# A planner's idea of TensorE and of the shared PSUM bank, corrected in a four-layer kernel

## The chip, the cores and the metric

The kernel runs on one core of one Trainium2 chip. The metric is the device time of one execution in microseconds. The kernel before takes 14,381.78 us in the median of three timed runs (14,376.06 to 14,391.36). Besides, one execution was recorded by the hardware profiler; all durations below come from it.

The core has five instruction queues, each worked off in order: PE (TensorE, matmuls), DVE (VectorE), ACT (ScalarE), POOL (GpSimd) and SP (SyncE, which only issues DMAs). The engines meet through semaphores.

## The reference

Four images of 64 x 64 positions with 128 channels (x is 4 x 64 x 64 x 128, f32) go through four layers. Layers 0 and 1 are state-space blocks: projections, a depthwise 3x3 convolution, and then a scan over all 4096 positions in four directions, with 16 states for every channel:

```
x_dbl = einsum('bkdl,kcd->bkcl', xs, x_proj_w)      # xs: the sequence in 4 directions
dts, Bs, Cs = split(x_dbl)                          # R rows, 16 rows, 16 rows
delta = softplus(einsum('bkrl,kdr->bkdl', dts, dt_w) + dt_b)
h = exp(delta * A) * h + (delta * x) * B            # one step of the scan, for each state
y = sum over the 16 states of h * C
```

The sums of the four directions are normalised, gated and projected. Layer 0 has 128 inner channels (R = 4) and a side branch of two full 3x3 convolutions; layer 1 has 256 inner channels (R = 8) and an MLP behind it. Layer 2 is a gated message from nine neighbours with two small MLPs, layer 3 a 7x7 neighbourhood attention. The change touches layers 0 and 1 alone.

## The kernel before, in words

Layers 0 and 1 of all images are computed in one stage, `scan_layers`. Its main line, `Scans.run` (L556), walks through 3072 units: 12 tasks (an image, a layer and a block of 128 channels), in each 16 steps (a direction and 1024 positions), in each step 16 units of 8 channels x 16 states on 128 partitions. For unit u the main line records: the DVE scan of unit u (L449) and, after every second unit, the DVE product with C (hc, L459); the POOL product of unit u+3 (h from dub and repB, L430); two bf16 matmuls and an exponential on ACT for unit u+2 (da, L438 and L440); every second unit the sums over states (yps, L530); now and then copies of y, the state and C on ACT. At the end of each unit's recording it issues the load of dub for unit u+7 on SP (L423). da has two PSUM buffers, so the matmuls of unit u+2 wait until scan u is done.

Two further streams of work are recorded in between, piece by piece, as Python generators wrapped in a `Lane`:

- **Preparation** (`Scans.prepare`, L314), lane "prep". It begins 22 units (`AHEAD`) before its step is used and has the 16 units of one step to finish; a slot r of a preparation is the unit r after its beginning. It projects xs into xd (f32 matmuls into ms, read by an ACT copy), stores xd to DRAM as xdd and loads it back repeated as repB and repC. Then it computes delta for two halves: a matmul into ms, read by an Abs (low) and a Relu (delta) on ACT; Exp, Ln, a sum on POOL make the softplus; a POOL product makes low = delta * x, which is stored to DRAM as dud (L388), from where every dub is loaded. Last it splits delta into three bf16 parts (parts), which twelve small DMAs (`own`, L400) copy into dp, the right-hand side of the decay matmuls. Of a second block of channels of the same image (`t.first` set) the projection is taken over from the first.
- **Side work** (`Side`), lane "side": everything else of layers 0 and 1, for other images than the one being scanned: projections, Silu with its two table loads, normalisations, depthwise and full convolutions, the MLP. Nearly all its matmuls are 512 columns wide, in f32.

Both streams share a single PSUM bank, tile ms (`bufs=1`, got through `bank()`, which makes the lane the `holder`). A matmul into ms must wait until ACT has read what was there; the holder is given up when the piece that reads it has been recorded.

What goes out when is decided by a planner at build time. `Plan` keeps for PE, ACT and POOL the time at which each would be done with what has been recorded (`at`), with a cost per instruction from `Counted` (all preparation and side instructions are recorded through it, at L97 in the profile). `Plan.slot` moves its clock by `UNIT` = 3.6 us per unit and books the main line's own work. Each generator yields a hint which engines its next piece uses ("PE", "ACT", "PE POOL", "TAB" for an activation with table loads); `Lane.fits` says yes if each of them could start early enough: start + `USUAL` must lie within the current slot plus `SLACK`. `Lane.ready` is the planned end of the lane's previous piece. `Lane.blocked` keeps a piece back that needs the bank while the other lane holds it; `Lane.step` first makes the holder record on until it lets go.

Preparation's pieces go out in a slot while they fit, and are forced out, fitting or not, while `pieces.count < rest - 1`, where `rest` is the slot r of the preparation. Side pieces go out as a credit allows, which grows by at least 0.83 pieces per unit; the longer they did not fit, the more lateness is allowed (0.06 us per piece of credit, up to 50 pieces).

Stores and reloads are not issued at once: `Plan.post` keeps them until the planned end of what they store (or a given due time) has passed, so that SP, which works in order, does not stand in front of the dub loads. Before the first dub load of a step all posts of "prep" are issued; at `rest == 0` all of "prep" and "rep".

Of the kernel before, what the change touches and what calls it, by code (L numbers as in the profile page):

```python
# [9 lines left out]
F32 = mybir.dt.float32  # L10
# [7 lines left out]
P = 128  # L18
# [10 lines left out]
HALVES = TS // T  # L29
# [44 lines left out]
class Counted:  # L74
# [5 lines left out]
    def __getattr__(self, name):  # L80
        call = getattr(self.engine, name)
        kind = self.kind

        def counted(*args, **kw):
            out = kw.get("out", args[0] if args else None)
            if kind == "PE":

                lhs, rhs = args[1:3]
                us = (4.0e-3 if rhs.dtype == F32 else 1.0e-3) * columns(rhs) * columns(lhs) / P
            elif kind == "ACT":  # L90
                us = 1.3 if name == "preload_act_table_set" else 0.2 + 0.85e-3 * columns(out)
                if kw.get("func", args[2] if len(args) > 2 else None) in (AF.Silu, AF.Gelu):
                    us += 1.3
            else:
                us = (1.0e-3 if name.startswith("tensor_scalar") else 2.3e-3) * columns(out)
            self.plan.enter(kind, us)
            return call(*args, **kw)  # L97

        return counted


def columns(t):
    return int(np.prod(t.shape[1:]))


UNIT = 3.6
USUAL = dict(PE=2.1, ACT=0.7, TAB=3.3, POOL=1.3)
SLACK = dict(PE=1.2, ACT=2.2, POOL=3.0)
LANDING = 8.0
FOUR_LANDING = 12.0  # L110
# [3 lines left out]
class Plan:  # L114
# [3 lines left out]
    def __init__(self, nc):  # L118
        self.nc = nc
        self.at = dict(PE=0.0, ACT=0.0, POOL=0.0)  # L120
        self.now, self.done = 0.0, 0.0
        self.posted, self.running = [], False

        self.lanes, self.holder = {}, None
        self.tensor = Counted(nc.tensor, self, "PE")
        self.scalar = Counted(nc.scalar, self, "ACT")
        self.gpsimd = Counted(nc.gpsimd, self, "POOL")
        self.vector, self.sync = nc.vector, nc.sync
# [36 lines left out]
class Lane:  # L165
# [4 lines left out]
    def __init__(self, plan, name, gen):  # L170
        self.plan, self.name, self.gen = plan, name, gen
        plan.lanes[name] = self
        self.next, self.ready, self.count = "", 0.0, 0

    def blocked(self):

        first = self.count == 0 or self.next.startswith("PE")
        return first and self.plan.holder not in (None, self.name)

    def fits(self, more=0.0):  # L180

        plan = self.plan
        if self.blocked():
            return False
        for what in self.next.split():
            if what == "SP":
                return self.ready <= plan.now
            kind = "ACT" if what == "TAB" else what
            start = max(plan.at[kind], self.ready)
            if start + USUAL[what] > plan.now + UNIT + SLACK[kind] + more:  # L190
                return False
        return True

    def step(self):

        plan = self.plan
        while self.blocked():
            plan.lanes[plan.holder].step()
        plan.done = max(self.ready, plan.now)
        reads = "ACT" in self.next or "TAB" in self.next  # L200
        try:
            self.next = next(self.gen)
        except StopIteration:
            return False
        finally:
            if reads and plan.holder == self.name:
                plan.holder = None
        self.ready = plan.done
        self.count += 1
        if isinstance(self.next, tuple):  # L210
            self.next, landed = self.next
            self.ready = max(self.ready, landed)
        return True
# [51 lines left out]
class Scans:  # L265
# [34 lines left out]
    def fetch(self, t):  # L300
# [6 lines left out]
        for c in range(NSTEP):  # L307
            for i, xc in enumerate(t.xc):
                cols = slice(c * TS, (c + 1) * TS)
                self.nc.sync.dma_start(out=xc[:, cols], in_=t.xcd[i][:, cols])  # L310
                yield

    def prepare(self, t, step):

        nc, W, half, post = self.plan, t.W, self.half, self.plan.post
        begin = self.plan.now
        k, c = t.steps[step]
        R = W.rank
        rows = R + 2 * NS

        xd = self.tile("xd", 1, shape=(P, T))
        if t.first is None:
            xdd = t.xdd[step] = self.dram.tile(
                [rows, TS], F32, name="xdd", tag=f"xdd{W.layer}", bufs=(4, 2 * len(t.steps))[W.layer]
            )
            ps = self.bank()
            for ti in range(W.nct):
                for i in range(HALVES):
                    nc.tensor.matmul(
                        image(ps[i * H : (i + 1) * H, :]),  # L330
                        W.xp[:, ti, k, :],
                        self.view(t.xc[ti], k, c, i, HALVES),
                        start=ti == 0,
                        stop=ti == W.nct - 1,
                    )
                yield "PE" if ti + 1 < W.nct else "ACT"
            nc.scalar.copy(xd, ps)

            def store_xd():
                for i in range(HALVES):  # L340
                    nc.sync.dma_start(out=xdd[:, half(i)], in_=xd[i * H : i * H + rows, :])

            post("prep", store_xd)
            ready = max(self.plan.done, self.plan.now) + LANDING
            yield "PE"
        else:
            xdd, ready = t.first.xdd[step], begin
            for i in range(HALVES):
                nc.sync.dma_start(out=xd[i * H : i * H + R, :], in_=xdd[0:R, half(i)])
            yield "PE", self.plan.now + LANDING  # L350
        out = t.prepared[step] = {}

        def repeat(i):
            rep = out["BC"[i]] = self.tile("rep" + "BC"[i], 2 - i)
            src = bass.AP(xdd.tensor, xdd.offset + (R + i * NS) * TS, [[TS, NS], [0, 8], [1, TS]])
            nc.sync.dma_start(out=rep, in_=src)

        for i, free in enumerate((5, 8)):
            post("rep", lambda i=i: repeat(i), max(begin + free * UNIT, ready))

        bias = W.dtb[:, k, t.ct : t.ct + 1]
        delta, low = self.tile("delta", 1), self.tile("low", 1)
        for i in range(HALVES):
            ps = self.bank()
            nc.tensor.matmul(
                ps,
                W.dtw[i * H : i * H + R, k, t.ct * P : (t.ct + 1) * P],
                xd[i * H : i * H + R, :],
                start=True,
                stop=True,  # L370
            )
            yield "ACT"
            nc.scalar.activation(low[:, half(i)], ps, AF.Abs, bias=bias)
            nc.scalar.activation(delta[:, half(i)], ps, AF.Relu, bias=bias)
            yield "PE" if i + 1 < HALVES else "ACT"
        nc.scalar.activation(low, low, AF.Exp, scale=-1.0)
        yield "ACT"
        nc.scalar.activation(low, low, AF.Ln, bias=1.0)
        yield "POOL"
        nc.gpsimd.tensor_add(delta, delta, low)  # L380
        yield "ACT POOL"
        parts = self.tile("parts", 1, shape=(P, 3, TS), dtype=BF16)
        nc.scalar.copy(parts[:, 0, :], delta)
        nc.gpsimd.tensor_mul(image(low), image(delta), self.view(t.xc[t.ct], k, c, 0, 1))
        yield "POOL"
        t.x_done = step == len(t.steps) - 1
        dud = out["du"] = self.dram.tile([P, TS], F32, name="dud", tag="dud", bufs=3)
        post("prep", lambda: nc.sync.dma_start(out=dud, in_=low))  # L388
        nc.gpsimd.tensor_sub(delta, delta, parts[:, 0, :])
        yield "ACT"  # L390
        nc.scalar.copy(parts[:, 1, :], delta)
        yield "POOL"
        nc.gpsimd.tensor_sub(parts[:, 2, :], delta, parts[:, 1, :])


        def own(part, j):
            if j == part == 0:
                out["delta"] = self.tile("dp", 2, shape=(96, 4, TS), dtype=BF16)
            nc.sync.dma_start(
                out=out["delta"][32 * part : 32 * part + 32, j, :], in_=parts[32 * j : 32 * j + 32, part, :]  # L400
            )

        for i in range(12):
            j, part = divmod(i, 3)
            post("rep", lambda part=part, j=j: own(part, j), begin + (9 + 0.7 * i) * UNIT)
        yield ""
# [143 lines left out]
    def run(self, between):  # L550

        total = NU * len(self.tasks)
        first = self.tasks[0]
# [6 lines left out]
        pieces, fetch, fetched = Lane(self.plan, "prep", iter(())), iter(()), 0  # L560
        for u in range(-7, total):
# [20 lines left out]
            ahead, rest = divmod(u + AHEAD, NG)  # L582
# [4 lines left out]
            if rest == 0 and 0 < ahead < total // NG:  # L587
# [7 lines left out]
                pieces = Lane(self.plan, "prep", self.prepare(self.tasks[n], step))  # L595
# [2 lines left out]
            if step == 0 and fetched < n < len(self.tasks) and self.tasks[n - 1].x_done:  # L598
                fetch, fetched = self.fetch(self.tasks[n]), n
            next(fetch, None)  # L600
            while (pieces.count < rest - 1 or pieces.fits()) and pieces.step():
                pass
            if u >= 0:
                n, i = divmod(u, NU)
# [1421 lines left out]
```

## Time and profile before

| what | us |
|---|---|
| median of three timed runs | 14,381.78 |
| the profiled execution, its own time | 14,374.6 |
| its span, first to last instruction | 14,372.8 |
| first scan begins | 199.5 |
| scan stage, 3072 units | 11,499 |
| DVE busy in the scan stage | 10,455 |
| one DVE scan, 128 x 1024 (L449, two forms) | 2.339 and 2.278 |
| one product with C, 128 x 2048 (L459) | 2.287 |
| one POOL product (L430) | 2.360 |
| one exponential (L440) | 1.088 |
| one table load on ACT | 1.283 |
| one 512-column f32 matmul into ms (L97) | 0.905 |

A waits row reads "engine, line, who ended the wait: total us, times, longest". PEld is PE's weight load; a matmul's wait often shows there, as the weight load of the same matmul is issued first. "issue" is time in which the engine waited for nothing that the profile shows. A row of the timeline has start, duration, engine, line, operation and what ended the idle time before it. All preparation and side instructions carry L97, the line of the wrapper, so they are told apart by their tiles: xd, low, delta, parts belong to preparation; o, d, sq, x, x2, hid, big and wts to side work; ms is the bank for both.

### The profile page before, as it was taken

To read this page: it belongs to the slowest core of one execution; us is meant where nothing else is said; L and a number is where in the kernel's file an instruction comes from. 1 tells how busy PE (TensorE), PEld (TensorE's weight loads), DVE (VectorE), ACT (ScalarE), POOL (GpSimd) and SP (SyncE) were. 2 spreads that over 40 slices of the span, in tenths; PEclk is the share of its full clock that TensorE was granted. 3 is DMA by queue.
4 is the path that set the end of the run, shared out by engine and by line. 5 is a ranking of instruction groups with operands and counts; after the bars stand their busy time and mean duration, and the time that the engine had idled before them with its cause. 6 is when DMAs were issued, how large, how long until landed. Compare 5 with 4: busy or idle time off the path is not lost. (4 is left out here: it accounts for less than half of the span.)

```text
span 14372.8 us, 120305 instructions
## 1 busy us (share of the span) xinstructions
PE 10333.4 (72%) x36408; PEld 2640.5 (18%) x36408; DVE 12073.0 (84%) x6647; ACT 8115.5 (56%) x10782; POOL 9870.5 (69%) x4606
## 2 busy tenths in 40 slices
PE   5776777677777767677776677777777766666999
PEld 1111111111111111111111111111111112113555
DVE  4988899988999889888989899999999954775666
ACT  3665546654666456654666555555555555553555
POOL 4777778877887778777887788888888852551000
PEclk7666676766677676767767677767776767777999
DMA  6878888888889888888888988788888841442000
GB/s 161 213 204 223 206 206 222 216 222 210 210 226 216 205 201 205 215 211 205 215 199 209 219 200 207 195 201 217 199 201 203 203 124 55 103 109 73 13 13 8
DMA packets 900351, 2567.23 MB, mean 179 GB/s; under 512 B 145271, under 2 KB 166911, under 8 KB 891511
## 3 DMA queue, kind: packets, MB, share of 16 engines
q1 hardware_dynamic: 899703, 2559.53, 71.9%
q8 instruction: 291, 4.77, 0.1%
q14 instruction: 357, 2.92, 0.1%
HBM read 2135.67 MB, written 272.37 MB: 168 GB/s over the span
## 5 line engine op out<-in xcount | busy, mean ns | idle before, releaser
L430 POOL TENSOR_TENSOR h<-dub,repB 128x1024 f32<-128x1024 f32 x3072 | 7180.8, 2360 | 1634.1 <-DMA dub<-dud 918.6
L449 DVE TENSOR_TENSOR_SCAN h<-da,state,h 128x1024 f32<-128x1024 f32 x2304 | 5321.1, 2339 | 698.1 <-ACT da L440 458.6
L440 ACT ACTIVATE da<-da,av 128x1024 f32<-128x1024 f32 x3072 | 3339.8, 1088 | 3559.9 <-PE da L438 3548.7
L438 PE MATMUL da<-dp,spread 96*128 96x512 bf16 x6144 | 2541.7, 508 | 2394.2 <-DVE h L449 2337.9
L459 DVE TENSOR_TENSOR hc<-h,C 128x2048 f32<-128x2048 f32 x1536 | 3513.2, 2287 | 111.1 <-ACT C L476 47.5
L530 PE MATMUL yps<-hc,gather 128*32 128x512 f32 x12288 | 2459.5, 886 | 5.6 <-DVE hc L459 5.6
L449 DVE TENSOR_TENSOR_SCAN h<-da,h 128x1024 f32<-128x1024 f32 x768 | 1728.7, 2278 | 417.4 <-POOL h L430 230.6
L438 PEld LDWEIGHTS <-spread 96*128 96x128 bf16 x6144 | 562.9, 108 | 5735.0 <-issue 5571.3
L97 PE MATMUL ms<-d,wts 128*128 128x512 f32 (+3 forms) x900 | 704.6, 905 | 297.7 <-ACT delta L97 92.9
L97 PE MATMUL ms<-xd,xpdt 8*128 8x512 f32 (+1 forms) x768 | 626.1, 906 | 285.7 <-ACT o L97 152.0
L97 ACT ACT_TABLE_LOAD x600 | 769.8, 1283 | 19.6 <-PE ms L97 8.8
L97 POOL TENSOR_TENSOR delta<-delta,low 128x1024 f32<-128x1024 f32 x192 | 451.8, 2353 | 259.7 <-ACT low L97 222.8
L97 ACT CAST parts<-delta 128x1024 bf16<-128x1024 f32 x384 | 399.9, 1041 | 296.6 <-POOL delta L97 277.7
L513 PE MATMUL yps<-y,ident 128*128 128x512 f32 x576 | 525.3, 1005 | 49.4 <-ACT y L540 48.8
L1805 ACT ACTIVATE s<-s,nmax 128x512 f32<-128x512 f32 x512 | 366.1, 717 | 250.2 <-DVE nmax L1802 244.0
L97 POOL TENSOR_TENSOR low<-delta,xc 128x1024 f32<-128x1024 f32 x192 | 501.9, 2614 | 3.5
L97 PE MATMUL ms<-pad,diag 96*32 96x504 f32 (+1 forms) x2304 | 409.0, 811 | 112.3 <-DMA pad<-xid 43.2
L1433 ACT ACTIVATE hid<-hid,relb 128x1024 f32<-128x1024 f32 x288 | 322.9, 1146 | 262.3 <-DVE hid L1428 262.1
L530 PEld LDWEIGHTS yps<-hc,gather 128*32 128x32 f32 x12288 | 283.1, 128 | 1011.1 <-issue 1002.8
L1535 POOL TENSOR_TENSOR acc<-acc,part 128x1024 f32<-128x1024 f32 x120 | 310.5, 2594 | 219.3 <-DVE part L1529 162.7
L1794 PE MATMUL sps<-k,q 32*128 32x512 f32 x1024 | 440.8, 659 | 21.1 <-DVE s L1801 21.1
L1428 DVE TENSOR_TENSOR hid<-cen,near 128x1024 f32<-128x1024 f32 x288 | 336.0, 1211 | 113.5 <-PE cen L1421 113.4
(275 smaller groups left out, 11295.8 us busy)
## 6 DMA issues: line engine op xcount, KB each, us to landing
dub<-dud SPq DMA_DIRECT2D x3072, 512.0 KB
dp<-parts SPq DMA_DIRECT2D x2304, 64.0 KB
repB<-xdd SPq DMA_DIRECT2D x192, 512.0 KB
repC<-xdd SPq DMA_DIRECT2D x192, 512.0 KB
dud<-low SPq DMA_DIRECT2D x192, 512.0 KB
spread<-gd SPq DMA_DIRECT2D x72, 1024.0 KB
pad<-xid SPq DMA_DIRECT2D x192, 256.0 KB
szd<-o SPq DMA_DIRECT2D x96, 256.0 KB
```

The lines of the kernel that those rows point to most:

```text
L97: return call(*args, **kw)
L430: self.nc.gpsimd.tensor_mul(dbu, self.live.pop(("dub", u)), t.prepared[step]["B"])
L438: self.nc.tensor.matmul(da[:, cols], self.C.spread[:, jj, :], dp[:, j, cols], start=True, stop=True)
L440: self.nc.scalar.activation(da, da, AF.Exp, scale=t.W.a[:, at : at + 1])
L449: nc.vector.tensor_tensor_scan(h[:, way], da[:, way], h[:, way], 0.0 if step % NSTEP == 0 else t.states[step - 1][:, u % NG : u % NG + 1], ...
L459: nc.vector.tensor_mul(hc, pair, t.prepared[step]["C"].unsqueeze(1).to_broadcast([P, 2, TS]))
L513: self.nc.tensor.matmul(self.like_part(yps, k), self.C.ident, self.part(t.y, k, c, b), start=True, stop=False)
L530: self.nc.tensor.matmul(out, self.C.gather[jj], rhs, start=False, stop=jj == 3)
L1428: nc.vector.tensor_add(hid.rearrange("p i (r w) -> p (i r) w", w=HW), cen[pair].rearrange("p i (r w) -> p (i r) w", w=HW), self.near[m][s] ...
L1433: nc.scalar.activation(hid, hid, AF.Gelu, bias=self.relb[:, m, t : t + 1])
L1794: nc.tensor.matmul(sps[:, h, :], q[ch, toks], k[ch, keys], start=True, stop=True)
L1805: nc.scalar.activation(s[:, i, :], s[:, i, :], AF.Exp, bias=nmax[:, h : h + 1], accum_out=total[:, h : h + 1],)
```

## The change

Six edits, all in the planner and in the order of recording. No instruction is added or removed.

1. In `Counted`, an f32 matmul is charged 2.4e-3 us per column instead of 4.0e-3; `USUAL["PE"]` becomes 1.4 instead of 2.1.
2. `Plan` has a new field `bank_free`: the planned end of the piece that last read the bank, written when the holder lets go.
3. `Lane.wants_bank` is new: the next piece begins with PE and the lane does not hold the bank. `blocked` uses it (before, a lane's very first piece also counted); `fits` starts such a piece no earlier than `bank_free`, and `step` plans its end from there.
4. `prepare` yields "PE ACT" before a matmul that is read at once, and no longer yields between that matmul and its reading: the copy into xd, and Abs and Relu of each half, are recorded in the same piece as their matmul. It now also yields once before its first matmul.
5. A preparation therefore has two pieces fewer behind its first matmul, and, where it makes its own projection, one more in front.
6. Preparation's pieces are forced while `pieces.count < rest - 4` instead of `rest - 1`.

```diff
-                us = (4.0e-3 if rhs.dtype == F32 else 1.0e-3) * columns(rhs) * columns(lhs) / P
+                us = (2.4e-3 if rhs.dtype == F32 else 1.0e-3) * columns(rhs) * columns(lhs) / P
...
-USUAL = dict(PE=2.1, ACT=0.7, TAB=3.3, POOL=1.3)
+USUAL = dict(PE=1.4, ACT=0.7, TAB=3.3, POOL=1.3)
...
-        self.lanes, self.holder = {}, None
+        self.lanes, self.holder, self.bank_free = {}, None, 0.0
...
+    def wants_bank(self):
+        return self.next.startswith("PE") and self.plan.holder != self.name
+
     def blocked(self):
-        first = self.count == 0 or self.next.startswith("PE")
-        return first and self.plan.holder not in (None, self.name)
+        return self.wants_bank() and self.plan.holder is not None
...
             start = max(plan.at[kind], self.ready)
+            if what == "PE" and self.wants_bank():
+                start = max(start, plan.bank_free)
             if start + USUAL[what] > plan.now + UNIT + SLACK[kind] + more:
...
-        plan.done = max(self.ready, plan.now)
+        plan.done = max(self.ready, plan.now, plan.bank_free if self.wants_bank() else 0.0)
...
             if reads and plan.holder == self.name:
-                plan.holder = None
+                plan.holder, plan.bank_free = None, plan.done
...
+        if t.first is None:
+            yield "PE" if W.nct > 1 else "PE ACT"
...
-                yield "PE" if ti + 1 < W.nct else "ACT"
+                if ti + 1 < W.nct:
+                    yield "PE ACT" if ti + 2 == W.nct else "PE"
             nc.scalar.copy(xd, ps)
...
-            yield "PE"
+            yield "PE ACT"
...
-            yield "PE", self.plan.now + LANDING
+            yield "PE ACT", self.plan.now + LANDING
...
-            yield "ACT"
             nc.scalar.activation(low[:, half(i)], ps, AF.Abs, bias=bias)
             nc.scalar.activation(delta[:, half(i)], ps, AF.Relu, bias=bias)
-            yield "PE" if i + 1 < HALVES else "ACT"
+            yield "PE ACT" if i + 1 < HALVES else "ACT"
...
-            while (pieces.count < rest - 1 or pieces.fits()) and pieces.step():
+            while (pieces.count < rest - 4 or pieces.fits()) and pieces.step():
                 pass
```

## The prediction

> **What bounds the kernel now.** The busy time by stretch comes first (columns: stretch, length, then busy us and count for PE, weight loads, DVE, ACT and POOL, then granted clock, DMA share, GB/s).
>
> ```profile
> 0.00:200.00 200.00, 99.54 (x274) 25.61 (x275) 4.09 (x21) 37.46 (x52) 20.62 (x29) 0.84 0.43 122
> 200.00:11699.00 11499.00, 8171.58 (x25558) 1700.54 (x25557) 10455.48 (x4620) 6644.59 (x8200) 9277.67 (x4270) 0.70 0.85 209
> ```
>
> The scan stage is 11,499 of the 14,372.8 us, and only there does the planner work; start and later layers are the same instructions in the same order. DVE is busy for 10,455 us of it: 3072 scans of 2.32 us and 1536 products of 2.29 us. The other 1,043 us are idle DVE, the most that any ordering can win. Whom DVE waits for is in the waits of that stretch:
>
> ```profile
> DVE h L449 <- ACT da L440: 609.4, 358, 10.4
> ...
> DVE h L449 <- POOL h L430: 399.6, 112, 183.0
> PEld ms L97 <- ACT delta L97: 388.5, 186, 5.3
> PEld ms L97 <- ACT o L97: 370.8, 159, 5.0
> ```
>
> 183.0 of the POOL row precede the first scan. Taking for each scan in the trace whichever input ended last, its exponential or its POOL product, 736 us belong to the exponential, 196 us to the product, and 111 us stand in front of hc (47.5 of it for C): together 1,043. In 298 scans (548 us) the exponential itself had waited for its matmul, so PE was late. The last two rows say why: matmuls into ms, the one bank that preparation and side work share, wait until ACT has read it. The timeline has one whole case:
>
> ```profile
> 2684.37 2.35 DVE L449 TENSOR_TENSOR_SCAN h<-da,state,h 128x1024 f32<-128x1024 f32 x1 [0.25 <-ACT da L440]
> ...
> 2686.48 0.69 ACT L97 ACTIVATE o<-ms,bias 128x512 f32<-128x512 f32 x1
> ...
> 2687.22 2.05 PE L97 MATMUL ms<-xd,xpdt 4*128 4x512 f32 x2 [2.72 <-ACT o L97]
> ...
> 2689.20 1.03 PE L438 MATMUL da<-dp,spread 96*128 96x512 bf16 x2
> ...
> 2690.27 1.09 ACT L440 ACTIVATE da<-da,av 128x1024 f32<-128x1024 f32 x1 [1.81 <-PE da L438]
> ...
> 2691.46 2.35 DVE L449 TENSOR_TENSOR_SCAN h<-da,state,h 128x1024 f32<-128x1024 f32 x1 [4.75 <-ACT da L440]
> ```
>
> Side's Silu into o (between two table loads) reads ms until 2687.17; preparation's matmul, already first on PE, starts only then; the scan's own decay matmul stands behind it; DVE stands for 4.75 us. The tile view of preparation's xd shows that this is the rule for its matmuls:
>
> ```profile
> its engine sat idle before it (us, times) until:
>   ACT o L97: 407.1, 173
>   ACT d L97: 145.9, 66
> ```
>
> **The change, part by part.** The order of instructions in both builds holds the same instructions, engine by engine (28,574 on PE, 10,272 on ACT, 4,611 on POOL, 6,649 on DVE, 7,998 on SP), so nothing is added or removed; places are. I call slot u the stretch of the recording in which scan(u) goes out. A piece recorded in slot u stands on PE ahead of decay(u+3), so scan u+3 feels it.
>
> *Fitting.* At 4.0e-3 us per column the plan charges a 512-column f32 matmul 2.05 us; the page has 905 ns. Its PE is thus booked out: counting placements without any time, 1,387 of preparation's 3,105 pieces went out by force and 2,323 of side's 2,570 only on credit. With 2.4e-3 (1.23 us) and USUAL 1.4 the counts are 146 of 3,210 and 776 of 2,564. By itself this has no price; it shows in the places below.
>
> *Hand-overs of the bank in one slot* (bank_free, and readings in the matmul's piece). I matched slots with the trace and took the mean exponential-caused idle in front of scan u+3. Preparation's matmul in the slot of side's reading: 1.98 us, 114 slots before, 14 after, saves 198. Side's after preparation's reading: 1.04 us, 165 to 115, saves 52. Side after side: 1.19 us, 7 to 26, costs 23. Preparation after preparation: 0 to 46, not in the trace. Its ends are 0.13 us (preparation's matmul and reading in one slot with no hand-over, 80 undisturbed slots) and 1.98; a hand-over without a table load is nearest to the 1.04 row, so 48 (6 to 91). Slots with bank matmuls but no such hand-over have 0.17 us; their number moves the sum by under 10. Net: -179. The remaining 115 were blind before and must now pass the plan's test; I keep their old price, with 0.17 as the other end (another -100).
>
> *One piece, "PE ACT".* ACT now has the reading queued right behind; what waits there is the next exponential, whose decay matmul is on PE behind the same matmul anyway, so the cover is PE's order. Bounds 0.03 (reading in the next slot, undisturbed) and 0.13 us: under 51 us for all 509 pieces; 0 taken, since 161 stood so already. But ACT bunches: by the durations of the rows, slots with over 3.3 us of ACT work besides the exponential rise from 195 to 232; such slots have 1.10 us of idle in front of the next scan against 0.30 (932/3072) for the mean scan: 37 x 0.80 = +30 (0 to 41).
>
> *Lag, and SP.* rest - 4 allows three pieces less, yet pieces that fit go earlier. The store of dud goes to SP in the median at slot 9 of its preparation instead of 14; its worst slot, 15, falls from 52 to 22 steps. The first three scans of a step cost 0.72 us of late POOL product where it was 15: saves 22. The twelve copies into dp stood in a single slot in 185 steps and now in 56; just behind such a burst dub arrives late, 0.62 us per step (114 us over 184): saves 80. If the queue has another reason the end is 0. POOL and DVE instructions do not change.
>
> *Sum.* -179 + 30 - 22 - 80 = -251 on the profiled execution's 14,374.6 us (1.8 us around its span): 14,124. It lies 7 us, 0.05%, below the median of the three timed runs, which I count as nothing. I predict 14,125. This is DVE idle, so it goes one to one, unless another input is late next: C and state (47.5 and 100.2 us of DVE waits) are, and I leave them as they are.
>
> **Rivals.** *A second wait right behind* (faster, less). DVE closer behind its inputs uncovers waits now hidden: POOL has 907.6 us of waiting for dub, of which only 196 us of product lateness reaches DVE, and DMA is at 0.85. If half the gain comes back: 14,250. Against it: the last two tasks took 921 us each against 958 on average, at a DMA share of 0.80 to 0.83.
>
> *SP holds dub back* (slower). These waits exist:
>
> ```profile
> SPq L423 <- DMA dud<-low: 559.2, 99, 17.1
> ...
> SPq L712 <- ACT o L97: 295.5, 86, 13.7
> ```
>
> Times are smaller in the plan, so stores are issued sooner after their producer: within one slot 177 of 191 dud stores (59 before) and 107 of 376 side stores (63). If one is not ready, SP stands (295.5/86 = 3.4 us) and every dub load behind it. That is 162 more. Each must cost DVE over 251/162 = 1.5 us to turn the sign; at the 1.98 us of the dearest row here: 14,124 + 321 = 14,445. Against it: dub is issued seven slots ahead and used in the fourth.
>
> *A slower TensorE.* The granted clock is 0.70 over the stage and by task between 0.64 and 0.74. At 0.64 PE's 2.66 us per scan would grow by 0.25 us; in all 1,575 slots with bank matmuls that is 394 us and 14,518. The rows say otherwise: the first task, at 0.64, took 964 us, one at 0.72 took 972. So 0 is taken.
> [...]
>
> *It does not do what it says* (no change): real slots take 3.74 us, not 3.6, so a plan of the bank could be off by as much as it avoids; hand-overs at old counts and prices: 14,375.
>
> *Better than the sum*: what remains is free too: 14,124 - 100 - 30 - 42 = 13,952.
>
> **How the numbers follow.** Forecast (gain 120 to 340) 0.58, better 0.11, second wait 0.16, no change 0.04, SP 0.08, clock 0.03. A measurement can tell about 0.2%, 29 us. Faster: 0.58 + 0.11 + 0.16 = 0.85; same 0.04; slower 0.11. The range runs from 13,950 (the better case) to 14,290 (most of the second wait's cases); outside lie no change, both slower cases and the ends, about 0.2.
>
> **What would show it.** Right: DVE idle in the scan stage from 1,043 to about 790 us at the same busy time; xd's idle for o and d from 553 us to under 150; the rows "PEld ms" for o and delta smaller; POOL's wait for dub below 850. Wrong: those rows gone but DVE waiting as long for POOL (second wait), SP rows for L712's and L388's successors above 500 us (SP), a clock under 0.66, or the ms rows unchanged (the plan's bank is not the real one).

## The result, and the profile after

The changed kernel takes 14,128.7 us in the median of four runs (14,123.32 to 14,152.81), the kernel before 14,378.92 us beside it: a ratio of 0.9829, with a 95% interval of 0.9812 to 0.9846, so 250 us less. The prediction was 14,125. The recorded execution is the longest of the four (span 14,151.0 us, 222 us less than the recorded one of before); below, traces are compared with traces and medians with medians.

The busy time by stretch of the changed kernel (columns as in the prediction):

```profile
0.00:200.00 200.00, 96.66 (x268) 25.17 (x269) 3.58 (x20) 35.79 (x49) 19.86 (x28) 0.82 0.42 121
200.00:11487.00 11287.00, 8094.94 (x25564) 1675.56 (x25563) 10465.36 (x4619) 6643.56 (x8203) 9269.05 (x4271) 0.71 0.87 212
```

Nearly the whole difference lies in the scan stage, 11,499 to 11,287 us. DVE is as busy as before (10,465 against 10,455 us), so it is idle DVE that went: 1,043 to 821 us. The waits of that stretch say where:

```profile
POOL h L436 <- DMA dub<-dud: 771.1, 321, 18.8
POOL delta L97 <- ACT low L97: 610.8, 119, 9.2
ACT low L97 <- PE ms L97: 519.6, 322, 12.0
DVE h L455 <- POOL h L436: 473.2, 158, 183.5
...
DVE h L455 <- ACT da L446: 307.7, 298, 10.2
...
PEld ms L97 <- ACT delta L97: 191.9, 142, 2.9
...
PEld ms L97 <- ACT o L97: 138.6, 99, 4.7
```

DVE's waiting for the exponential halved (609.4 to 307.7), and the two rows of matmuls that wait for the bank fell from 388.5 and 370.8 to 191.9 and 138.6. But DVE's waiting for POOL grew (399.6 to 473.2, 183.5 of it again ahead of the first scan). Preparation's own matmuls, in the tile view of xd, hardly wait for side's readings now (407.1 and 145.9 before):

```profile
its engine sat idle before it (us, times) until:
  ACT da L446: 172.6, 111
...
  ACT o L97: 55.0, 45
...
  ACT d L97: 20.7, 10
```

By what ended last before each scan, as the prediction counts it:

| idle DVE in the scan stage, us | before | predicted change | after | change |
|---|---|---|---|---|
| the exponential last | 736 | -149 | 397 | -339 |
| the POOL product last | 196 | -102 | 282 | +86 |
| in front of hc | 111 | 0 | 139 | +28 |
| together (gaps under 0.1 us in the sum only) | 1,043 | -251 | 821 | -222 |

The sum came out, the terms did not: the first gained more than twice what was expected, the second turned its sign, and the third, put at nothing, cost 28 us (the wait of hc for C alone grew from 47.5 to 80.3 us). That the total was met within 4 us is therefore luck; that idle DVE in this stage would fall, and behind exponentials above all, is not.

### The profile page after: what moved, and what is told of

It reads as the page before. It is cut to its first block, busy times and chain, and to the rows that moved or that the text cites. A ratio compares the mean times of both kernels' runs of the same rounds, so it can differ in the third digit from the quotient of the medians.

```text
span 14151.0 us, 120242 instructions
## 1 busy us (share of the span) xinstructions
PE 10247.9 (72%) x36408; PEld 2607.7 (18%) x36408; DVE 12084.3 (85%) x6647; ACT 8111.5 (57%) x10782; POOL 9862.8 (70%) x4606
## 5 line engine op out<-in xcount | busy, mean ns | idle before, releaser
L436 POOL TENSOR_TENSOR h<-dub,repB 128x1024 f32<-128x1024 f32 x3072 | 7173.7, 2357 | 1146.2 <-DMA dub<-dud 771.1
L465 DVE TENSOR_TENSOR hc<-h,C 128x2048 f32<-128x2048 f32 x1536 | 3513.6, 2288 | 139.4 <-ACT C L482 80.3
L97 ACT CAST parts<-delta 128x1024 bf16<-128x1024 f32 x384 | 400.6, 1043 | 363.2 <-POOL delta L97 348.9
L97 ACT ACTIVATE low<-ms,av 128x512 f32<-128x512 f32 x384 | 263.9, 687 | 529.5 <-PE ms L97 523.9
```

The source lines that it names most:

```text
L436: self.nc.gpsimd.tensor_mul(dbu, self.live.pop(("dub", u)), t.prepared[step]["B"])
L465: nc.vector.tensor_mul(hc, pair, t.prepared[step]["C"].unsqueeze(1).to_broadcast([P, 2, TS]))
```

## The experiments

All edits are shown against the kernel before or the changed kernel, whichever the label's text names. Each ratio is to runs of the kernel before that were timed beside it on the same chip (medians 14,379.92 us for the first four rows, 14,390.4 for the next four and 14,389.2 for the last three).

| kernel | median us | ratio to before | 95% interval |
|---|---|---|---|
| costs alone | 14,324.0 | 0.9963 | 0.9950 to 0.9976 |
| bank_free alone | 14,567.5 | 1.0122 | 1.0105 to 1.0139 |
| changed, old costs | 14,515.0 | 1.0091 | 1.0075 to 1.0106 |
| changed, no bank_free | 14,291.1 | 0.9937 | 0.9922 to 0.9952 |
| bank_free and 3.2e-3 | 14,206.5 | 0.9874 | 0.9860 to 0.9889 |
| bank_free and costs | 14,114.2 | 0.9809 | 0.9792 to 0.9825 |
| changed, 3.7 us per unit | 14,094.5 | 0.9797 | 0.9782 to 0.9812 |
| changed, dp copies in a burst | 14,211.7 | 0.9878 | 0.9863 to 0.9893 |
| changed, every second dub | 13,768.1 | 0.9570 | 0.9556 to 0.9584 |
| changed, dub load first | 14,259.8 | 0.9914 | 0.9898 to 0.9931 |
| bank_free, costs, 3.7 us per unit | 14,028.7 | 0.9750 | 0.9736 to 0.9765 |

### Which of the edits carries it

The bank theory is the prediction's: what counts is how often the bank goes from one lane to another within a slot. Its rival is that only the plan's booking counts. Four kernels take the two edits apart.

Costs alone, on the kernel before:

```diff
-                us = (4.0e-3 if rhs.dtype == F32 else 1.0e-3) * columns(rhs) * columns(lhs) / P
+                us = (2.4e-3 if rhs.dtype == F32 else 1.0e-3) * columns(rhs) * columns(lhs) / P
-USUAL = dict(PE=2.1, ACT=0.7, TAB=3.3, POOL=1.3)
+USUAL = dict(PE=1.4, ACT=0.7, TAB=3.3, POOL=1.3)
```

> The kernel before with the corrected matmul costs alone (2.4e-3 us per column, USUAL PE 1.4). Bank theory (time follows the hand-overs of the bank in one slot, at the prices read in the trace of before): preparation after side falls from 114 to 35 (-156 us), side after preparation rises from 165 to 181 (+17), side after side 8 to 25 (+20), preparation after preparation 0 to 40 (+42), bursts of dp copies 185 to 45 (-87), dud at slot 15 from 52 to 2 steps (-36): -200, about 14,180 us. Fit theory (what counts is that pieces fit and go early, the bank's field adds nothing; forced preparation pieces 1,387 to 130): like the full change, about 14,130 us.

bank_free alone, on the kernel before (its pieces are the old ones, so the test of a lane's first piece stays):

```diff
+    def wants_bank(self):
+        first = self.count == 0 or self.next.startswith("PE")
+        return first and self.plan.holder != self.name
...
+            if what == "PE" and self.wants_bank():
+                start = max(start, plan.bank_free)
...
+        plan.done = max(self.ready, plan.now, plan.bank_free if self.wants_bank() else 0.0)
...
+                plan.holder, plan.bank_free = None, plan.done
```

> The kernel before with bank_free alone, old costs, old pieces, rest - 1. Bank theory: hand-overs 114 to 91 (-46 us) and 165 to 49 (-121), bursts 190 as before, dud at slot 15 from 52 to 63 (+8): about 14,220 us. Fit theory: 1,665 of 3,084 preparation pieces still forced, 2,438 of 2,564 side pieces not fitting: no gain, about 14,380 us.

The changed kernel with the old costs is the first diff undone; the changed kernel without bank_free takes out what looks at it:

```diff
-            if what == "PE" and self.wants_bank():
-                start = max(start, plan.bank_free)
...
-        plan.done = max(self.ready, plan.now, plan.bank_free if self.wants_bank() else 0.0)
+        plan.done = max(self.ready, plan.now)
```

> The changed kernel with the old costs (4.0e-3, USUAL PE 2.1). Bank theory: 79 and 80 hand-overs (-69 and -88 us against before), bursts 189 as before, dud at slot 15 in 132 steps (+58): about 14,280 us. Fit theory: 1,438 of 2,515 pieces forced as before: about 14,380 us.

> The changed kernel without bank_free (neither fits nor step look at it). Bank theory: preparation after side stays at 14 (-198 us against before) but side after preparation rises to 236 (+74), preparation after preparation 51 (+53), side after side 29 (+25), bursts 46 (-86), dud at slot 15 in 15 steps (-27): about 14,220 us. Fit theory: fewer forced pieces than in the changed kernel (77 against 146): 14,130 us or less.

Measured: 14,324, 14,567, 14,515 and 14,291. No theory had this. The costs alone are worth 56 us, not 200 or 250; bank_free alone, which was to save 160 or nothing, costs 188. The waits of DVE in that kernel have the reason in one row:

```profile
DVE h L455 <- ACT da L446: 913.2, 298, 418.5
```

The last number is a single wait of 418.5 us. The busy times around it, in the kernel with bank_free alone:

```profile
11430.00:11856.00 426.00, 244.54 (x310) 72.53 (x303) 7.37 (x4) 132.01 (x172) 71.76 (x58) 0.63 0.10 31
```

DVE works 7 of 426 us. Side work has to be over 16 units before the end of the scan stage; with the old costs and the bank's time the plan is so booked out that side pieces fall behind, and in unit 3056 the remaining 289 are forced out in one heap, ahead of the next decay matmul. In the changed kernel with the old costs it is 224 pieces, and the longest wait is 324.1 us. In the kernel before, no unit has more than 6. Without these single waits the two would be at 14,149 and 14,191.

That is only arithmetic, so a kernel with bank_free and no heap was run. Its only other difference to bank_free alone is this cost:

```diff
-                us = (4.0e-3 if rhs.dtype == F32 else 1.0e-3) * columns(rhs) * columns(lhs) / P
+                us = (3.2e-3 if rhs.dtype == F32 else 1.0e-3) * columns(rhs) * columns(lhs) / P
```

> The kernel before with bank_free and a half-corrected cost (3.2e-3, USUAL PE stays 2.1), old pieces, rest - 1. The one that only cures the heap at the end of the stage: in the kernel with bank_free alone 289 side pieces went out by force in unit 3056 and DVE stood 418.5 us there; here no unit has more than 6 and side work ends at unit 3041. Heap theory (bank_free alone is worth its gain, the costs only keep side work in time): 14,567 - 418 = about 14,150 us. Other theory (the right costs are a gain of their own, and the slow run of bank_free alone shows that the field itself does harm): above 14,300 us.

It took 14,206 us: 57 more than the heap theory's number, but 361 less than bank_free alone for a cost changed by a fifth, and no wait of DVE for an exponential is longer than 9.8 us. So the heap does the harm, not the field. (A cost of 3.2e-3 without the field was not run, so how much of the 14,206 us is the cost's own is open.)

Then both edits, the first two diffs together, without the one-piece matmuls and the lag:

> The kernel before with bank_free and the corrected costs, but old pieces and rest - 1 (the changed kernel without its one-piece matmuls and its lag). Hand-overs in one slot 40, 39, 28, 39 against 14, 115, 26, 46; bursts of dp copies 60 against 56; dud at slot 15 in 6 steps against 22. If one piece and lag add nothing: 14,130 us, as the changed kernel, or a little less. If they carry a part of the gain: 14,200 us or more.

14,114 us, beside 14,129 for the whole change, whose interval overlaps. So bank_free is worth 210 us beside the right costs (14,324 to 14,114) and 162 us inside the whole change (14,291 to 14,129), the costs are worth 56 alone, and the one-piece matmuls with rest - 4 add nothing at 3.6 us per unit. (rest - 4 alone on the old pieces is not possible: a step's dud would not yet exist when its first load is issued.)

Why bank_free helps can be read from the hand-overs. The table tells them by the tiles in the traces: slot u ends on PE at the decay matmuls of unit u+3 and on ACT at the exponential of unit u+3, and a hand-over is a matmul into ms that follows, in the same slot, the reading of what ms held before. The price is the mean exponential-caused idle in front of scan u+3. (The prediction and the expectations have other counts; "Why the prediction was right" says where they come from.)

| kernel | side after preparation: slots, us each | preparation after side | preparation after preparation |
|---|---|---|---|
| before | 202, 0.98 | 132, 2.02 | none |
| costs alone | 201, 0.90 | 44, 2.30 | 44, 0.14 |
| changed, no bank_free | 187, 0.95 | 14, 1.60 | 51, 0.01 |
| bank_free and costs | 64, 0.63 | 46, 1.59 | 39, 0.07 |
| changed | 39, 0.68 | 14, 1.40 | 46, 0.09 |

The field takes most of side's matmuls out of the slots in which preparation has just read the bank: 39 and 64 slots with it, 187 to 202 without. Those that remain look cheaper as well, but in the changed kernel the mean of 0.68 us has a standard error of 0.33, so this is not shown. Preparation's matmuls become fewer in side's slots already by the costs, and stay dear. The costs alone win little all the same: in their trace the idle time in front of hc is 173 us instead of 111, and slots with bank matmuls but no hand-over cost 214 us instead of 156.

### Why POOL products are late

The prediction had them late behind bursts of dp copies and late stores of dud, and expected 102 us back; 86 more were lost. Three kernels ask why.

All twelve dp copies held to the last slot again:

```diff
-            post("rep", lambda part=part, j=j: own(part, j), begin + (9 + 0.7 * i) * UNIT)
+            post("rep", lambda part=part, j=j: own(part, j), begin + 15.9 * UNIT)
```

> The changed kernel with all twelve dp copies held to the last slot again (191 steps instead of 56), nothing else moved. Burst theory, at the 0.62 us read in the trace of before: 135 x 0.62 = +84 us, 14,213 us; at the 1.28 us that a burst has in the trace of the changed kernel: +150 us, 14,280. If bursts do not matter: 14,130 us.

14,211.7 us, 83 more than the changed kernel, where the price read before the change gave 84. But the late products hardly carry it (289 against 282 us of idle DVE); POOL waits 933.1 us for dub instead of 771.1, and of the trace's 51 us more idle DVE 38 stand behind exponentials, 7 behind products and 6 in front of hc. So bursts cost time, but not by the mechanism that the price stood for, and that the numbers agree is luck. How the burst gets there is not shown; the matmuls' own waiting for dp hardly grew (78 to 83 us).

The price itself was read at the wrong place. Its 114 us are the product-caused idle of five scans of each step, from the scan before the burst's slot to the third one behind it. In the trace of before, 107 us of them belong to products that POOL had finished before SP issued the first copy of the burst (63 of 72 us in the trace of the changed kernel), so these products were late for another reason.

Every second dub load left out:

```diff
+        if u % 2:
+            self.live["dub", u] = self.live["dub", u - 1]
+            return
```

> The changed kernel with only every second dub loaded; the odd units multiply with the dub of the unit before, so half of the products are of the wrong channels (work left out: 1,536 of 3,072 dub loads). Order, pieces and all other instructions stay. Transfer theory (late POOL products come from dub still on its way): POOL's 771 us of waiting for dub fall under 150, POOL-late DVE idle 282 to under 80 us, about 13,930 us. Queue theory (POOL's own pieces hold it up, which stood 611 us for preparation's low): POOL-late idle stays over 200 us, about 14,100 us.

13,768 us, 361 less than the changed kernel. Its POOL waits in the scan stage:

```profile
POOL delta L97 <- ACT low L97: 725.4, 134, 10.0
POOL h L439 <- ACT state L479: 436.1, 171, 8.1
POOL h L439 <- DMA dub<-dud: 150.4, 42, 15.3
```

The wait for dub is down to 150.4 us and product-caused idle to 33 us, while POOL stands even longer for preparation's low (725.4): that wait is hidden, the wait for dub is not. The queue theory falls. The trace of the changed kernel says the same: followed back on POOL to the last wait, 256 of its 282 us of product-caused idle begin with a wait for dub (175 of 196 us before). Exponential-caused idle fell too, from 397 to 287 us.

Why dub arrives late is not settled by this kernel, as it changes two things. The DMA share fell from 0.87 to 0.58; but the five buffers of dub now also hold ten units, so SP hardly stands for a free buffer any more (209.1 us; 4,210.0 in the changed kernel) and issues a load 20.0 us ahead of its product in the median instead of 13.7. Fewer bytes and earlier issue were not tried apart.

Can the order of the transfers help? Each unit's dub load issued ahead of that unit's stores:

```diff
+            if 0 <= u + 7 < total:
+                self.load(u + 7)
             even, eighth, first_one = u % 2 == 0, u % 8 == 1, u % NG == 0
...
-            if 0 <= u + 7 < total:
-                self.load(u + 7)
```

> The changed kernel with the dub load of each unit issued ahead of that unit's stores and pieces on SP instead of behind them. If stores that are issued too early hold dub back on SP (210 us for o, 176 for xd, 89 for sq in the waits of SP): POOL-late idle 282 to under 200 us, about 14,050 us. If SP has the slack of its four units: 14,130 us.

14,260 us: slower by 131. The waits of DVE and of PE in that kernel:

```profile
DVE h L455 <- ACT da L446: 543.5, 369, 12.0
DVE h L455 <- POOL h L436: 271.9, 75, 184.8
```

```profile
PE ms L97 <- DMA pad<-xid: 240.2, 40, 12.3
PE ms L97 <- ACT sq L97: 155.9, 64, 15.1
```

SP's first row in that kernel, and then in the changed one:

```profile
SPq L429 <- POOL h L436: 4718.8, 1871, 13.4
```

```profile
SPq L429 <- POOL h L436: 4210.0, 1746, 13.3
```

Half of the expectation was right: issued ahead of the stores, dub comes earlier, and product-caused idle fell from 282 to 72 us, with as many bytes to move. But SP now stands at dub, for the buffer that POOL still reads (4,718.8 us against 4,210.0), in front of everything else: matmuls wait 240.2 us for side's pad instead of 128.6, and idle DVE behind exponentials that had waited for their matmul is 367 us instead of 150.

### A faster version

The plan's clock moves 3.6 us per unit; the changed kernel needs 3.67.

```diff
-UNIT = 3.6
+UNIT = 3.7
```

> The changed kernel with the plan's clock at 3.7 us per unit instead of 3.6; its real units take 3.67 (11,287 us / 3072). Forced preparation pieces 146 to 63, side after preparation 115 to 78, preparation after side 14 to 8, bursts of dp copies 56 to 24, dud at slot 15 in 22 to 5 steps. If late POOL products come from the late stores and bursts: POOL-late idle 282 to about 200 us, 14,050 us. If they come from DVE's closeness alone: 14,110 us or more.

14,094.5 us: product-caused idle is 201 us, the number of the late-store theory, hc's falls to 112 and exponential-caused idle rises from 397 to 431. The medians gain 34 us, less than the 80 expected; the traces differ by 78, as the changed kernel's is its longest execution and this one the shortest. Then bank_free and the costs alone, with 3.7:

> bank_free and the corrected costs on the kernel before (old pieces, rest - 1), with 3.7 us per unit. Hand-overs in one slot 29 + 21 + 12 + 37 = 99 (changed kernel 201, with 3.7 alone 139), bursts 24, dud at slot 15 in 1 step. If the two gains add (14,114 and 14,094 us against 14,129): about 14,080 us or less. If the clock of the plan is worth something only with the one-piece matmuls: 14,114 us.

14,028.7 us, 2.5% below the kernel before and 100 us below the changed one, and better than its parts added (14,080). Its trace has 685 us of idle DVE: 161 behind products, 109 in front of hc. With 3.7 us per unit the one-piece matmuls and the lag are together a loss of 66 us (14,094.5 against 14,028.7), and the two intervals lie apart; which of the two it is was not tried.

## Why the prediction was right

The forecast was right in sign and size, and right that hand-overs of the bank are where the gain is. Inside its sum the terms were off by more than 100 us each and cancelled. Of its signs, the bank's came as said: idle DVE at 821 us, xd's idle for o and d at 75.7 us, the two ms rows halved, POOL's wait for dub at 771.1. So did the sign of the second wait: DVE waits longer for POOL than before.

- *What bounds the kernel.* Right. DVE's busy time stayed within 10 us, and its idle time fell by 222 us, as much as the span did.
- *Fitting has no price by itself.* Half right. Costs alone give 56 us. What the step missed is that bank_free without them starves side work until it comes out in one heap; the two edits together gain 276 us (14,390.4 to 14,114.2), and bank_free alone loses 188.
- *Hand-overs, -179.* Right in kind; the counts are the step that failed. The prediction's counts come out if pieces are told by the hints that they yield. A preparation's first piece of before carries no hint, so it was missed; and behind a "PE ACT" piece of the changed kernel the Exp, which doesn't read the bank, passed for a reading. Told by the tiles, side after preparation went from 202 slots to 39, not from 165 to 115, and preparation after side from 132 to 14, not from 114 to 14. In the traces, all slots with hand-overs together fell from 474 to 58 us. The other wrong size is preparation after preparation, 0.09 us each instead of 1.04. A part was lost again: slots with bank matmuls but no hand-over became more and dearer (1,189 at 0.13 us, then 1,435 at 0.20), which is 131 us more where the prediction had under 10; why is not shown.
- *ACT bunching, +30.* It didn't cost that: slots with 3.3 to 4.5 us of other ACT work have 0.14 us of idle in front of scan u+3 in the new trace, against 0.93 before. Of the 204 such slots of before, 62 held a hand-over and had 2.28 us; the other 142 had 0.34. So most of the price was the hand-overs', counted twice.
- *Lag and SP, -102.* Wrong in sign as far as products go, +86. At the five scans that the prediction put down to bursts the idle time fell from 114 to 93 us, but little of it was the bursts' (above). Behind dud stores at slot 15 it fell from 37 to 27 us, behind those at slot 14 it rose from 3 to 34, and the rest is spread over all units of a step. This is the second-wait rival beside the gain: POOL's wait for dub became shorter (907.6 to 771.1 us), but DVE, closer behind, feels more of it.
- *One piece, 0.* Right on its place in the sum: leaving the pieces and the lag out moves the time by 15 us at 3.6. The waits it makes are there (ACT for ms before low, 97.7 to 519.6 us; POOL for low, 185.1 to 610.8) and are hidden at that clock of the plan; at 3.7 the pieces and the lag lose 66 us.
- *A slower TensorE* did not happen: the granted clock is 0.71 against 0.70.
- *SP holds dub back* did not turn the sign, but it is not ruled out as a part of the 86 us. The two rows that the prediction named fell; a third, for xd's store, rose from 43.5 us:

```profile
SPq L429 <- DMA dud<-low: 277.2, 40, 12.9
...
SPq L718 <- ACT o L97: 210.0, 71, 9.3
SPq L348 <- ACT xd L97: 175.9, 50, 9.5
```

The kernel with the dub load first shows that what stands ahead of dub on SP has a part in the late products of the changed kernel; the kernel before was not run with that order.

## What to carry to other kernels

A planner needs the resource that its lanes share, not only the engines: one field that says when a single-buffered PSUM bank is free was worth 210 us here beside the right costs. Check what a stricter plan does to the work that it postpones: look for one long wait at a deadline before judging the edit by its time. Count events by what is written and read, not by the labels of the pieces that do it: here the labels showed a fall from 165 to 115 slots where it was one from 202 to 39. And before a price is put down to a cause, see that the cause comes first: most of the idle time put down to bursts stood behind products that were done when the burst began.

## What was not expected of the hardware

In a stage with 16 DMA engines at a share of 0.87 and DVE 93% busy, leaving out 1,536 of the 3,072 loads of dub (512 KB each) took 361 us off, while issuing all of them ahead of their unit's stores on SP cost 131 us. In these two kernels dub came earlier both times (POOL's wait for it fell from 771.1 to 150.4 and 686.1 us); in the second, what stood behind it on the queue paid for it: the matmuls' wait for pad rose from 128.6 to 240.2 us.
